# A graph layer with masked attention on one core: nine gathered slots instead of ten, two PSUM banks for the sorting step, and a later norm

## The chip, the cores and the metric

The kernel runs on one core of a Trainium2 chip. The metric is device time in microseconds of one execution, smaller is better. A core has five engines that take their instructions in order, each from its own queue: TensorE (PE in the profile, its weight loads PEld), VectorE (DVE), ScalarE (ACT), GpSimd (POOL) and SyncE (SP). Transfers are issued from SP, ACT and POOL.

## The reference

Two layers over 4096 nodes with 512 features; `adj` is 4096 x 4096, with a full diagonal and otherwise 0.2% of entries that are not zero, all below one.

```python
# layer 0
a = adj + eye
d = sum(a, axis=1) ** -0.5
out = relu((d[:, None] * a * d[None, :]) @ x @ W.T + b)
x = layernorm(x + out)
# layer 1: attention over the neighbours of adj
scores = q @ k.T * kd ** -0.5 + 0.01 * eye - 1e16 * (1 - max(adj, eye))
x = layernorm(x + softmax(scores) @ v @ Wo)
```

In layer 1 every entry of `adj` below one is pushed down by at least 1e16 times its distance from one, so the softmax falls on the diagonal alone, as long as no edge weight reaches one and q, k are not huge. Then layer 1 is `layernorm(x + x @ (Wv Wo))`.

## The kernel before

The function `few_edges_below_one` computes this short form and a flag `bad`, which is one where its conditions do not hold (an edge of weight one or more, a row with more edges than its tables take, large keys). Where `bad` is set, a second function, `general`, computes everything densely; the branch is at L414 and L415.

The 4096 rows are 32 row tiles of 128. **First pass** (loop over `t`, up to `first.close()`): each row tile of `adj` (2 MB) is loaded once; ACT sums its rows (L682); PE computes `x @ W.T` (L675), ACT scales it by `d` (L702) and POOL writes it to DRAM as `y` (L704). VectorE begins to extract the edges: for each of eight segments of 512 columns the eight largest values and their places (MAX8 at L731, FIND_INDEX8 at L732), then a chain of short instructions (L735 to L793) that leaves up to K = 24 edges of every row in a record `rec`. Twelve `early` tiles and five `resident` ones are extracted from the first load; the other fifteen (`again`) are loaded a second time during the second pass, when a buffer of the pool `big` is free (`reload`, L535).

**Sorting step** (`match_key` to `match_end`). A row has some 8 edges, but some have 21. The second pass gathers KH = 10 rows of `y` per row, so a row with more edges lends them to lanes of rows with few. The rows of a tile are put in order of their number of edges: a key per row (L808/L810), a transpose of the key by PE (`match_across`, L815), a count of the keys above (`match_ranks`, L822 on ACT in the second pass, L824 before), permutation matrices (`match_perm`, L832, one for the row itself and one for each of the routes), small products that move the fields of the records (`match_move`, L840 for the row itself, L843 for each route), and `match_end` (L851 to L858), which adds the parts up into columns `cols_all` and weights `wr_all`. Keys and moved fields share one PSUM tile, `bank`, made once: columns 0 to 127 for the key, the next 70 for the fields. The dictionary in the loop tells at which slot `k` of an iteration each stage is issued.

**Second pass** (loop over `i`, 30 tiles of ten slots, then the last two). For each slot POOL gathers 128 rows of `y` (`gather`, L1057, an indirect DMA of 256 KB, AHEAD = 18 slots ahead), ACT builds a 128 x 128 matrix from the weights (`spread`: L955, L959 for the far slots, L965, L968 for the `SAME` = 5 near ones), and PE multiplies (L1265; each fp32 product shows as two records). The last two tiles (`SUMMED`) add their near slots up first (`presum`) and use fewer products (L1084). `own_part` (L1115, ACT) and `own_bias` (L1119) add the diagonal and the bias; `scaled` (L1126) and `residual` (L1137) give the tile's layer 0 output. Then, by the tables `near` and `far` in `at` (tiles behind, slot): T transposes (L663) and copies to SBUF (L668), M multiplies with `Wv Wo` (L675), Q sums squares (L1145), V adds the variance (L1156) and, for two tiles together, takes the power -1/2 on POOL (L1164), F scales (L1170) and writes the result from ACT's queue (L1171). `load_own` (L1067, L540) loads a tile's own rows of `y` and `x` on SP, two tiles ahead, in three buffers.

```python
        far = {"T": (2, 0), "M": (2, 6), "Q": (3, 1), "V": (3, 4), "F": (3, 8)}
                match(*{1: (RANKS,), 3: (MOVE, PERM), 6: (END,), 7: (KEY,), 9: (ACROSS,)}.get(k, ()))
```

The order of the source is not wholly that of the engines: instructions of different chains are placed on an engine when the program is built, and extraction, which nothing else holds back, is placed ahead of the pace that the loop sets (`shares`, 28 tiles). PSUM has eight banks: two for transposes (`pt`), one `bank`, five accumulators (`acc`).

Of the kernel before, what the change touches and what calls it, by code (L numbers as in the profile page):

```python
# [9 lines left out]
FP = mybir.dt.float32  # L10
# [409 lines left out]
def few_edges_below_one(  # L420
# [32 lines left out]
    KH = 10  # L453

    ROUTES = ((112, 10, 14), (120, 14, 19), (76, 19, 24))
    SAME = KH - max(hi - lo for _, lo, hi in ROUTES)

# [9 lines left out]
    ps_a = ctx.enter_context(tc.tile_pool(name="ps_a", bufs=5, space=bass.MemoryType.PSUM))  # L467
# [34 lines left out]
    for n, (c, _, _) in enumerate(ROUTES):  # L502
        ranks(sources[:, n + 1, : c + 1], -2, 2 * c + 1 - P)
        ranks(sources[:, n + 1, c + 1 :], -2, P - 1)
# [205 lines left out]
    def extraction(t, a_t, rec):  # L710
# [35 lines left out]
        def drop(f, r):  # L746
# [19 lines left out]
                lambda: nc.scalar.activation(  # L766
                    mask, keyf[:, 0], AF.Sign, accum_out=n_all[:, t : t + 1]
                ) if second else nc.vector.tensor_scalar(
                    mask, keyf[:, 0], 0.0, 0.0, op0=ALU.is_gt, op1=ALU.add,
                    accum_out=n_all[:, t : t + 1],  # L770
                ),
# [28 lines left out]
    bank = ps_t.tile([P, 512], FP, name="bank", bufs=1)  # L800
# [12 lines left out]
    def match_across(key):  # L813
        pk = bank[:, :P]
        tc.keep_in_program_order(nc.tensor.transpose(pk, key.to_broadcast([P, P]), ident))  # L815
        return pk
# [18 lines left out]
    def match_move(rec, perm):  # L835

        r = upper(rec)
        merged = bank[:, P : P + 7 * KH].rearrange("p (f k) -> p f k", f=7)
        tc.keep_in_program_order(
            nc.tensor.matmul(merged, perm[:, 0], r[:, :, :KH], start=True, stop=False)  # L840
        )
        for n, (_, lo, hi) in enumerate(ROUTES):
            nc.tensor.matmul(  # L843
                merged[:, :, KH - (hi - lo) :], perm[:, n + 1], r[:, :, hi - 1 : lo - 1 : -1],
                start=False, stop=(n == len(ROUTES) - 1),
            )
        return merged

    def match_end(t, merged):
        wr = wr_all[:, t]  # L850
        nc.vector.tensor_copy(wr[:, 0:3], merged[:, 0:3])  # L851
        nc.vector.tensor_tensor(wr[:, 0:3], wr[:, 0:3], merged[:, 3:6], ALU.add)
        nc.vector.tensor_tensor(wr[:, 1], wr[:, 1], merged[:, 6], ALU.add)
        nc.vector.tensor_scalar(cols_all[:, t], wr[:, 0], float(N - 1), None, op0=ALU.min)
        if second:
            nc.scalar.activation(wr[:, 3], wr[:, 1], AF.Copy, scale=-1.0)
        else:
            nc.vector.tensor_scalar(wr[:, 3], wr[:, 1], -1.0, None, op0=ALU.mult)  # L858
# [188 lines left out]
    AHEAD = 18  # L1047
# [14 lines left out]
    def load_own(i):  # L1062
        if i >= NT:
            return
        t = order[i]
        yo[i] = p2.tile([P, D], FP, name="yo", bufs=3)
        nc.sync.dma_start(yo[i], y[ts(t, P), :])  # L1067
        xs[i] = load_x(t, nc.sync, p2, 3)
# [42 lines left out]
    def own_part(i):  # L1111
        t = order[i]
        own = own_all[:, t : t + 1]
        d = d_all[:, t : t + 1]
        nc.scalar.activation(own, own, AF.Identity, scale=d, bias=d)  # L1115
# [15 lines left out]
    def residual(i, c=slice(0, D), part=0):  # L1131
        if i % 2 == 0 and i not in sts:
            sts[i] = small.tile([P, 2, 5], FP, name="sums")
            sts[i + 1] = sts[i][:, 1]
            pairs[i] = sts[i]
            sts[i] = sts[i][:, 0]
        nc.vector.scalar_tensor_tensor(  # L1137
            hs[i][:, c], hs[i][:, c], 0.0, xs[i][:, c], op0=ALU.max, op1=ALU.add,
            accum_out=sts[i][:, part : part + 1],
        )  # L1140
# [19 lines left out]
    def power(i, n):  # L1160

        j = i % 2
        st = pairs[i - j][:, j : j + n]
        nc.gpsimd.tensor_tensor(  # L1164
            st[:, :, 4], st[:, :, 3], mhalf.to_broadcast([P, n]) if n > 1 else mhalf, ALU.pow
        )
# [39 lines left out]
    yo, zs, hs, pts, hTs, ws, sts, pairs, mats, halves = ({} for _ in range(10))  # L1206
# [4 lines left out]
    load_own(1)  # L1211
    own_part(0)
# [8 lines left out]
    def at(step, i, k):  # L1221

        near = {"T": (1, 5), "M": (1, 8), "Q": (2, 2), "V": (2, 3), "F": (2, 7)}
        far = {"T": (2, 0), "M": (2, 6), "Q": (3, 1), "V": (3, 4), "F": (3, 8)}
        for table, tiles in ((near, range(NT - 2, NT)), (far, range(NT - 2))):
            behind, place = table[step]
            if k == place and i - behind in tiles:
                return i - behind
        return None

    for i in range(NT + 2):
# [5 lines left out]
        for k in range(KH):  # L1237
            ends = p == NT - 1
            t = at("T", i, k)
            if t not in (None, NT - 1):  # L1240
                hTs[t] = evacuate(p2, "hT", transpose_rows(hs[t]))
            t = at("M", i, k)
            if t not in (None, NT - 1):
                ws[t] = times(hTs.pop(t), wvo)
            if i == NT - 1:
# [3 lines left out]
                if k == 7:  # L1249
                    scaled(i, HALVES[0])  # L1250
                    residual(i, HALVES[0])
                if k == 8:
                    pts[i] = transpose_rows(hs[i], (0, 1))
                if k == 9:
                    for n in range(KH - SAME + 1):
                        summed_products(i, n, HALVES[1])
                    hTs[i] = p2.tile([P, ND, P], FP, name="hT", bufs=2)
                    nc.scalar.copy(
                        hTs[i][:, 0:2].rearrange("p c s -> p (c s)"), pts[i][:, : 2 * P]
                    )  # L1260
# [11 lines left out]
            if i + 1 in SUMMED and k >= 5:  # L1272
                presum(i + 1, k - 5)
# [15 lines left out]
            if k == 2:  # L1289
                load_own(i + 2)  # L1290
            if k == 3 and i + 1 < NT:
                own_part(i + 1)
            t = at("Q", i, k)
            if t is not None:
                squares(ws[t], D**-0.5, sts[t][:, 3:4])

            t = at("V", i, k)
            if t is not None:
                variance(t)
                if t >= NT - 2:  # L1300
                    power(t, 1)
                elif t % 2:
                    power(t - 1, 2)
            if k == 6 and i < NT:
                own_bias(i)
            if k == 6 and has_p:
                eps_var(p)
            t = at("F", i, k)
            if t is not None and (t >= NT - 2 or t % 2):
                if t < NT - 2:  # L1310
                    finish(t - 1)
                finish(t)
            if k in (3, 9):
                scan_half()
            if staged[KEY] < NT - 2:
                match(*{1: (RANKS,), 3: (MOVE, PERM), 6: (END,), 7: (KEY,), 9: (ACROSS,)}.get(k, ()))
            elif k % 2:
                match(*ALL)
            if k == 9 and queue and len(reloaded) < free:
                reload()  # L1320
            while k == 1 and i + 2 < NT and order[i + 2] not in matched:
# [33 lines left out]
```

## Time and profile before

| | us |
|---|---|
| median of three runs | 749.92 (746.94 to 760.13) |
| the profiled execution | 746.64 |
| its span, first to last instruction | 744.8 |
| PE busy in the span | 591.2 |
| VectorE busy | 545.4 |
| ACT busy | 525.2 |
| POOL busy | 393.2 |

The span is one execution, and all durations are from it. "Busy" is the time in which an engine has an instruction under way; instructions that only wait, branch or issue a transfer do not count. A group's line shows its source line, engine, operation, what it writes and reads, its count, then busy time and mean duration in ns, then the idle time of the engine just before its instructions and who ended most of that. A wait is named after the semaphore that came last, and "issue" or "remote" stands where the records do not tell it. The profile was taken over 744.8 us in which 230.5 MB were moved, 310 GB/s on average.

### The profile page before, as it was taken

How to read it: one execution, taken by the hardware profiler on the slowest of the kernel's cores; microseconds unless marked ns; L12 is line 12 of the kernel's file. 1: busy time of each engine (PE TensorE's matmuls, PEld its weight loads, DVE VectorE, ACT ScalarE, POOL GpSimd, SP SyncE). 2: the span in 40 equal slices, each digit the busy share in tenths (PEclk: the TensorE clock that was granted, in tenths of full speed). 3: DMA queues.
4: the chain of work that ended last, by engine and by line, in shares of the span. 5: the costliest groups of instructions: out<-in, count | busy, mean ns of one | idle time of the engine just before them, and what ended most of it. 6: DMA issues, size and time to landing. Idle time of an engine off the chain costs nothing. (4 is left out here: it accounts for less than half of the span.)

```text
span 744.8 us, 8023 instructions
## 1 busy us (share of the span) xinstructions
PE 591.2 (79%) x1638; PEld 273.9 (37%) x1638; DVE 545.4 (73%) x2109; ACT 525.2 (71%) x1152; POOL 393.2 (53%) x494
## 2 busy tenths in 40 slices
PE   1799959867815687989979699979996789898692
PEld 0444424433302233434434344434442334343350
DVE  6779899999997289889978799959994443322410
ACT  1787798958975287688958597867884887773432
POOL 3224233322337656766666666666665566667500
PEclk9999999999967778999999899999998899999896
DMA  8999999999947689999999988989996577777601
GB/s 341 403 422 426 425 423 406 421 430 413 423 187 262 198 294 366 343 371 373 380 305 343 325 300 313 337 297 333 351 333 209 171 221 239 224 240 248 199 24 62
DMA packets 54411, 230.54 MB, mean 310 GB/s; under 512 B 8592, under 2 KB 9616, under 8 KB 48080
## 3 DMA queue, kind: packets, MB, share of 16 engines
q0 software_dynamic: 30800, 100.95, 40.6%
q1 hardware_dynamic: 18416, 119.55, 40.5%
q10 hardware_dynamic: 5136, 9.44, 3.4%
q14 instruction: 44, 0.36, 0.1%
q8 instruction: 15, 0.25, 0.1%
HBM read 213.12 MB, written 16.78 MB: 309 GB/s over the span
## 5 line engine op out<-in xcount | busy, mean ns | idle before, releaser
L1057 POOL DMA_INDIRECT g<-y,cols_all x320 | 312.9, 978 | 151.0 <-issue 82.6
L1265 PE MATMUL acc<-g,s_t 128*128 128x512 f32 x600 | 283.6, 619 | 20.0 <-ACT s_t L959 20.0
L731 DVE MAX8 v_all<-a_t 128x8 f32<-128x512 f32 x256 | 168.8, 679 | 18.1 <-DMA a_t<-in_adj_dram 18.1
L732 DVE FIND_INDEX8 idx<-v_all,a_t 128x8 uint32<-128x512 f32 x256 | 174.0, 683 | 0.0
L1265 PEld LDWEIGHTS acc<-g,s_t 128*128 128x128 f32 x600 | 116.2, 200 | 151.9 <-issue 124.4
L675 PE MATMUL acc<-wvo,hT 128*128 128x512 f32 x256 | 125.4, 630 | 25.4 <-issue 14.8
L675 PE MATMUL acc<-wT,xT 128*128 128x512 f32 x256 | 121.7, 621 | 16.4 <-ACT xT L668 12.2
L687 ACT ACTIVATE dump<-a_t 128x2048 uint8<-128x2048 f32 (+1 forms) x52 | 119.5, 2297 | 0.0
L675 PEld LDWEIGHTS acc<-wvo,hT 128*128 128x128 f32 x256 | 49.1, 200 | 87.6 <-issue 71.9
L675 PEld LDWEIGHTS acc<-wT,xT 128*128 128x128 f32 x256 | 48.3, 198 | 72.3 <-issue 50.2
L955 ACT ACTIVATE sq<-cols,wr_all 128x128 f32<-128x128 f32 x192 | 66.9, 391 | 9.9 <-issue 7.3
L959 ACT ACTIVATE s_t<-sq,wr_all 128x128 f32<-128x128 f32 x160 | 72.0, 483 | 1.6 <-ACT sq L955 1.2
L968 ACT ACTIVATE s_t<-s_t,wr_all 128x128 f32<-128x128 f32 x150 | 52.4, 391 | 4.6 <-issue 3.8
L682 ACT ACTIVATE dump<-a_n 128x4096 uint8<-128x4096 f32 x15 | 54.5, 3632 | 0.3 <-DMA a_n<-in_adj_dram 0.3
L744 DVE MAX8 top<-key 128x8 f32<-128x64 f32 x192 | 39.0, 214 | 12.1 <-issue 7.3
L1119 DVE SCALAR_TENSOR_TENSOR yo<-yo,own_all,b_bc 128x512 f32<-128x512 f32 x32 | 23.8, 744 | 24.1 <-DMA yo<-y 10.4
L1126 DVE SCALAR_TENSOR_TENSOR h<-acc,d_all,yo 128x512 f32<-128x512 f32 (+1 forms) x33 | 23.9, 724 | 23.5 <-PE acc L1265 11.3
L540 POOL DMA_DIRECT2D x_t<-in_x_dram x32 | 17.9, 564 | 41.2 <-PE pt L663 41.0
L694 POOL TENSOR_SCALAR deg<-deg_all 128x1 f32<-128x1 f32 x32 | 6.7, 220 | 62.4 <-ACT dump L682 62.3
L704 POOL DMA_DIRECT2D y<-y_t x32 | 19.0, 593 | 38.6 <-ACT y_t L702 38.1
L702 ACT ACTIVATE y_t<-acc,d_all 128x512 f32<-128x512 f32 x32 | 21.6, 686 | 22.6 <-POOL d_all L697 16.7
L815 PE MATMUL bank<-ident,rank_key 128*128 128x128 f32 x32 | 10.2, 320 | 33.4 <-issue 11.5
(123 smaller groups left out, 651.5 us busy)
## 6 DMA issues: line engine op xcount, KB each, us to landing
a_t<-in_adj_dram SPq DMA_DIRECT2D x30, 2048.0 KB
a_n<-in_adj_dram SPq DMA_DIRECT2D x15, 2048.0 KB
x_t<-in_x_dram POOLq DMA_DIRECT2D x32, 256.0 KB
y<-y_t POOLq DMA_DIRECT2D x32, 256.0 KB
yo<-y SPq DMA_DIRECT2D x32, 256.0 KB
x_t<-in_x_dram SPq DMA_DIRECT2D x32, 256.0 KB
out_dram<-r_t ACTq DMA_DIRECT2D x32, 256.0 KB
g<-y,cols_all POOLq DMA_INDIRECT x320
```

The source lines that it names most:

```text
L675: nc.tensor.matmul(u, srcT[:, dc, :], w[:, dc, :], start=(dc == 0), stop=(dc == ND - 1))
L682: nc.scalar.activation(dump[:, : part.shape[1]], part, AF.Copy, accum_out=dst)
L687: nc.scalar.activation(dump[:, o], a_t[:, o], AF.Relu, scale=-1.0, accum_out=neg_all[:, t, halves[0] : halves[0] + 1],)
L731: long.append(lambda o=o, seg=seg: nc.vector.max(v[:, o], seg))
L732: long.append(lambda o=o, seg=seg: nc.vector.max_index(idx[:, o], v[:, o], seg))
L744: return lambda: nc.vector.max(top[:, f, r * 8 : r * 8 + 8], keyf[:, f])
L955: nc.scalar.activation(sq, cols1, AF.Square, bias=wr[:, 2, k : k + 1])
L959: nc.scalar.activation(s_t[:, k, :], away(), AF.Relu, scale=wr[:, 3, k : k + 1], bias=wr[:, 1, k : k + 1],)
L968: nc.scalar.activation(s_t[:, k, :], s_t[:, KH, :], AF.Copy, scale=wr[:, 1, k : k + 1])
L1057: nc.gpsimd.indirect_dma_start(out=slots[j], out_offset=None, in_=y[:, :], in_offset=bass.IndirectOffsetOnAxis(ap=cols_all[:, t, k : k + 1 ...
L1126: nc.vector.scalar_tensor_tensor(hs[i][:, c], zs[i][:, c], d_all[:, order[i] : order[i] + 1], yo[i][:, c], op0=ALU.mult, op1=ALU.add,)
L1265: nc.tensor.matmul(zs[i], mats[i][:, k, :], slots.pop(i * KH + k), start=(k == 0), stop=(k == KH - 1),)
```

## The change

KH goes from ten to nine, with a new table of routes: four routes instead of three, each made of runs of lanes (first lane, last lane, rank of the row that fills the first) instead of one start lane. The matrices `sources` are filled accordingly. The shared `bank` becomes two tiles in a bank each, `pk` and `pm`, and the accumulators go from five banks to four. Three small ACT operations go to VectorE. The norm's power is taken for each tile, and the last step (F) follows an iteration later; other steps move by a slot or more, with the copy (E) apart from the transposes (T), and the variance's first part (S) in the table. Own rows are loaded three tiles ahead, in four buffers. The lines on `HALVES` and on the last iterations that only follow the shorter tile are left out below.

```diff
-    KH = 10
-    ROUTES = ((112, 10, 14), (120, 14, 19), (76, 19, 24))
-    SAME = KH - max(hi - lo for _, lo, hi in ROUTES)
+    KH = 9
+    ROUTES = (
+        (9, 13, ((62, 79, 54), (82, 89, 36), (91, 94, 28), (96, 96, 24), (99, 101, 23),
+                 (104, 107, 20), (110, 112, 16), (114, 127, 13))),
+        (13, 16, ((63, 65, 10), (66, 68, 13), (74, 75, 15), (80, 81, 7), (95, 95, 5), (97, 98, 4),
+                  (102, 103, 2), (108, 108, 0))),
+        (16, 20, ((61, 61, 4), (66, 66, 2), (90, 90, 1), (109, 109, 3), (113, 113, 0))),
+        (20, 24, ((109, 109, 0),)),
+    )
+    SAME = KH - max(hi - lo for lo, hi, _ in ROUTES)
...
-    ps_a = ctx.enter_context(tc.tile_pool(name="ps_a", bufs=5, space=bass.MemoryType.PSUM))
+    ps_a = ctx.enter_context(tc.tile_pool(name="ps_a", bufs=4, space=bass.MemoryType.PSUM))
...
-    for n, (c, _, _) in enumerate(ROUTES):
-        ranks(sources[:, n + 1, : c + 1], -2, 2 * c + 1 - P)
-        ranks(sources[:, n + 1, c + 1 :], -2, P - 1)
+    nc.gpsimd.memset(sources[:, 1:], float(P))
+    for n, (_, _, runs) in enumerate(ROUTES):
+        for a, b, r in runs:
+            ranks(sources[:, n + 1, a : b + 1], -2, 2 * r + 1 - P)
...
-                lambda: nc.scalar.activation(
-                    mask, keyf[:, 0], AF.Sign, accum_out=n_all[:, t : t + 1]
-                ) if second else nc.vector.tensor_scalar(
-                    mask, keyf[:, 0], 0.0, 0.0, op0=ALU.is_gt, op1=ALU.add,
-                    accum_out=n_all[:, t : t + 1],
-                ),
+                one(mask, keyf[:, 0], 0.0, 0.0, op0=ALU.is_gt, op1=ALU.add,
+                    accum_out=n_all[:, t : t + 1]),
...
-    bank = ps_t.tile([P, 512], FP, name="bank", bufs=1)
...
-        pk = bank[:, :P]
+        pk = ps_t.tile([P, 512], FP, name="pk", bufs=1)[:, :P]
...
-        merged = bank[:, P : P + 7 * KH].rearrange("p (f k) -> p f k", f=7)
+        pm = ps_t.tile([P, 512], FP, name="pm", bufs=1)
+        merged = pm[:, : 7 * KH].rearrange("p (f k) -> p f k", f=7)
...
-        if second:
-            nc.scalar.activation(wr[:, 3], wr[:, 1], AF.Copy, scale=-1.0)
-        else:
-            nc.vector.tensor_scalar(wr[:, 3], wr[:, 1], -1.0, None, op0=ALU.mult)
+        nc.vector.tensor_scalar(wr[:, 3], wr[:, 1], -1.0, None, op0=ALU.mult)
...
-    AHEAD = 18
+    AHEAD = 16
...
-        yo[i] = p2.tile([P, D], FP, name="yo", bufs=3)
+        yo[i] = p2.tile([P, D], FP, name="yo", bufs=4)
         nc.sync.dma_start(yo[i], y[ts(t, P), :])
-        xs[i] = load_x(t, nc.sync, p2, 3)
+        xs[i] = load_x(t, nc.sync, p2, 4)
...
-        nc.scalar.activation(own, own, AF.Identity, scale=d, bias=d)
+        nc.vector.tensor_scalar(own, own, 1.0, d_all[:, t : t + 1], op0=ALU.add, op1=ALU.mult)
...
-    def power(i, n):
-        j = i % 2
-        st = pairs[i - j][:, j : j + n]
-        nc.gpsimd.tensor_tensor(
-            st[:, :, 4], st[:, :, 3], mhalf.to_broadcast([P, n]) if n > 1 else mhalf, ALU.pow
-        )
+    def power(i):
+        st = sts[i]
+        nc.gpsimd.tensor_tensor(st[:, 4:5], st[:, 3:4], mhalf, ALU.pow)
...
+    load_own(2)
...
-        near = {"T": (1, 5), "M": (1, 8), "Q": (2, 2), "V": (2, 3), "F": (2, 7)}
-        far = {"T": (2, 0), "M": (2, 6), "Q": (3, 1), "V": (3, 4), "F": (3, 8)}
+        near = {"T": (1, 5), "E": (1, 5), "M": (1, 8), "S": (1, 6), "Q": (2, 2), "V": (2, 3), "F": (2, 7)}
+        far = {"T": (2, 0), "E": (2, 3), "M": (2, 7), "S": (2, 1), "Q": (3, 0), "V": (3, 3), "F": (4, 3)}
...
             if k == 2:
-                load_own(i + 2)
+                load_own(i + 3)
...
-            if k == 6 and i < NT:
+            if k == 4 and i < NT:
                 own_bias(i)
-            if k == 6 and has_p:
-                eps_var(p)
+            for t in at("S", i, k):
+                eps_var(t)
...
-                match(*{1: (RANKS,), 3: (MOVE, PERM), 6: (END,), 7: (KEY,), 9: (ACROSS,)}.get(k, ()))
+                match(*{2: (RANKS,), 4: (MOVE,), 5: (PERM, KEY), 8: (ACROSS, END)}.get(k, ()))
...
-            while k == 1 and i + 2 < NT and order[i + 2] not in matched:
+            soon = i + 3 if (i, k) == (NT - 4, KH - 1) else i + 2
+            while k in (1, KH - 1) and soon < NT and order[soon] not in matched:
                 some(count[0] + 1)
                 match(*ALL)
```

## The prediction

> **What bounds it now.** I read the page's first part, then the busy time by stretch. The bounds of the stretches come from the timeline: every twentieth L1265 product starts a row tile, so 228.3 us is the first product, 285.1 that of tile 3, 554.7 that of tile 21, 704.4 the end of tile 29. Columns: stretch, its length, busy time of each engine, granted clock, DMA share, GB/s.
>
> ```profile
> 0.00:228.30 228.30, 161.44 (x497) 78.20 (x497) 209.06 (x872) 171.44 (x172) 72.91 (x163) 0.95 0.96 392
> 228.30:285.10 56.80, 38.98 (x88) 17.29 (x89) 34.79 (x123) 29.18 (x78) 37.73 (x39) 0.80 0.78 262
> 285.10:554.70 269.60, 241.30 (x652) 108.98 (x652) 238.23 (x872) 212.57 (x593) 181.07 (x187) 0.96 0.94 336
> 554.70:704.40 149.70, 123.22 (x321) 55.09 (x320) 56.94 (x221) 100.40 (x284) 98.41 (x103) 0.93 0.72 222
> 704.40:744.80 40.40, 26.23 (x86) 14.35 (x84) 6.39 (x24) 11.56 (x28) 3.11 (x5) 0.86 0.16 55
> ```
>
> The first pass is a transfer (DMA 0.96). In the 476.1 us from 228.3 to 704.4 PE leads: 403.5 us busy, 72.6 idle, 15.9 per tile. In the longest stretch VectorE is close behind (13.2 us a tile to PE's 13.4, of 15.0); afterwards it is nearly idle, because extraction (L731, L732) is done at 578. Then PE's own waits after 222 us (total, times, longest); and below them three groups by form (busy, mean ns | idle before):
>
> ```profile
> PE bank L815 <- issue: 11.5, 3, 6.7
> PE bank L815 <- DVE wr_all L853: 6.9, 2, 4.5
> PE bank L815 <- ACT dump L1145: 6.2, 1, 6.2
> PE bank L815 <- DVE idx L732: 4.7, 1, 4.7
> PE bank L840 <- ACT above L822: 3.7, 2, 2.2
> PE bank L840 <- issue: 2.6, 1, 2.6
> PE bank L815 <- DVE v_all L731: 1.7, 1, 1.7
> ```
> ```profile
> L1057 POOL DMA_INDIRECT g<-y,cols_all x320 | 312.9, 978 | 151.0 <-issue 82.6 <-PE acc L1265 34.4 <-remote 14.1
> L1265 PE MATMUL acc<-g,s_t 128*128 128x512 f32 x600 | 283.6, 619 | 20.0 <-ACT s_t L959 20.0
> L832 DVE TENSOR_SCALAR perm<-sources,rank 128x512 bf16<-128x512 bf16 x32 | 11.5, 359 | 13.3 <-issue 10.2 <-ACT s_t L965 2.5 <-ACT above L822 0.5
> ```
>
> L815 sums to 31.0 us; L840, with three smaller rows (1.2, 1.1, 1.0), to 9.6. So 40.6 of the 72.6 us that PE stands idle end at the two instructions that write the tile `bank`. At 283.95 the key transpose starts right after VectorE's last read of the *other* half of that bank (L853, 283.74); everything behind it on PE, products included, stood 4.46 us. Gathers aren't the limit: POOL waits 34.4 us for PE to free a slot, PE 6.2 us for a gather.
>
> **What the skill says.** PSUM — Partial Sum Buffer, "PSUM bank collisions raise a hardware error": two engines are kept apart by bank, not by address; that is the wait just shown. TensorE: Matmul & The Clock Gate, Part 1: an idle window of about 3.4 us halves the clock; the trace agrees (0.80 granted where the 4 to 7 us waits lie, 0.96 later). SBUF — State Buffer, "Who interferes with whom": VectorE in a two-port mode and GpSimd lock each other out. The trace hints at it: after `perm` at 418.20 and 569.21 VectorE starts nothing for 4.1 and 4.6 us while gathers issue; in other places nothing follows.
>
> **The change, part by part.**
>
> *Nine slots.* 60 fewer L1265 records at 283.6/600 = 0.473 us: −28.4 us of PE work, 0.95 a tile; the two summed tiles lose a slot each (L1084, 2 records of 0.44 and 4 of 0.24): −2 in the tail. POOL loses 32 gathers of 0.98 + 0.30 issue (−41 us); ACT 32 × (391 + 483 ns) = −28; the DMA engines 32 × 262 kB = 8.4 of 230 MB. PE is the bound, so the 28.4 counts; the rest is hidden behind PE today. 16 instead of 18 gathers ahead is 1.8 tiles either way. Counting the reference's rows (at most 21 edges beside the diagonal) through the new table, every edge finds a free slot and none is hit twice, so the `general` branch isn't taken.
>
> *Fourth route.* One more small product (L843, 0.19 us, 0.04 to 0.06 apart in a run) per tile: +2 on PE. `perm` grows from 512 to 640 columns: 359 × 5/4 = +0.09 us. 16 more iotas (seven took 1.10 us) and a memset (0.2): POOL's first x load goes 2.7 us later than 3.39, hidden, since x is first transposed after W's second transposes (20.5); uncovered it would cost 2.7.
>
> *Two banks.* Takes the cause of the 40.6 us away. PE then waits at L815 only for the key and for ACT's reading of the last one (L822), at L840 for `perm` and L853. New places (PERM a slot behind MOVE, END four slots behind MOVE instead of three) leave more room. Bounds: all 40.6 and some 10 us of clock, or 10 if VectorE is late in its place. Price paid: accumulators 5 to 4. In the loop's order a bank for the second product (M, i−2 at slot 7) is the one that r_t of tile i−4 frees at slot 3: four slots of 1.4 us. In the first pass PE waits 3.9 us for ACT today; the DMA share of 1.00 (to 206 us) hides it: 0, at most +4.
>
> *ACT to VectorE.* own_part (32 × 378 ns on ACT; 0.20 on VectorE by its one-column rows), mask (18 × 0.28), sign (24 × 0.19), `perm`: 6.4 + 5.0 + 4.6 + 2.9 = +19 us on VectorE, 0.6 a tile. It ends VectorE's waits for ACT (own 8.8, mask 8.5). In the long stretch VectorE would need 13.8 us a tile. Own and sign may be two-port operations, some 55 more beside the 72 of today (`perm`, L851, L854); three of those were followed by 2.5 to 4.6 us of nothing, so +3 to +10; I take 3, as part falls in the idle stretch.
>
> *Norm later, one tile at a time.* T stays, the hT copy comes three slots later (ACT waited 20.6 us for the products ahead of it), M one later, final scale 4 tiles behind. POOL: 30 powers of 0.556 for 15 of 0.749, +5.5 us against −41. A power waits for VectorE's variance with the gathers queued behind it (11.4 us before 705); the gathers' lead of 16 covers that. Output transfers are the same, only the last two tiles set the end, and theirs stay near: 0.
>
> *Own rows.* Two 256 KB loads a tile, a tile earlier, a buffer more. SP's queue is in order: from 223.8 to 262.9 it waits for VectorE's h with the first reload behind. The fourth load now goes at once, so reloads may start up to 15 us sooner; they aren't on the path (one 1.6 us wait for a_t after 228). VectorE's waits for yo (10.4 us, three) mostly end. One more pair at the start competes with the first gathers: 0.5 MB at 300 GB/s (estimate from the second stretch), +1 to +2, taken +1.
>
> **Sum by stretch.** First 56.8: slots 2.8, half of its three bank waits (4.7 + 6.7 + 4.5): −11. Long stretch: the most VectorE allows at 13.8 is 18 × 1.2 = 21, and 6 more if extraction, which the compiled order ran ahead, spreads into the idle stretch: −27. Third: slots 8.5, bank 3, hT and own rows 2.5: −14. Tail −2, start +1, locks +3. Total −50: 746.6 − 50 = **697 us**. That is against the profiled execution (746.64, span 744.8); it stood 3.3 below the median of the runs (749.92), so I expect the median at 697 to 700 and give 697.
>
> **Rivals.**
> - *All of it* (0.22): bank waits wholly gone, clock back. 746.6 − 28.4 − 40.6 − 10 + 2 − 2 + 3 = 670. For: VectorE idles 93 of 150 us in the third stretch, POOL's floor is 288 × 1.28 + 17 = 386. Against: VectorE's order.
> - *The wait moves to VectorE* (0.22): the long stretch stays VectorE's, L851 still waits in its line for the moved fields; only the slots count where PE leads. 746.6 − 28 + 3 = 722. For: 88% busy and 0.6 a tile more.
> - *Within 2%* (0.07): the same with a slow start and more locks, about 740.
> - *The accumulators* (0.05, slower): r_t waits for POOL's power (12.0 us in four waits, up to 6.3). If it comes over four slots (5.8 us) late, PE stops at M. To eat 50 us over 28 tiles it must be 1.8 + 5.8 = 7.6 us late each time; at 9 us, 28 × 3.2 = 90: 697 + 90 = 787.
> - My forecast has 0.44, its own range 680 to 714.
>
> The range 663 to 729 leaves out the accumulators, most of the within-2% case and the edges of the first two. About 2% is what a measurement of this kernel can tell from no change (limits 735 and 765): faster 0.86, same 0.09, slower 0.05.
>
> **What would show it.** PE's L815 and L840 waits together under 12 us; 540 L1265 records and about 254 us busy; 288 gathers; VectorE over 13.5 us a tile in the long stretch, with extraction ending later in tiles than 21; PE's clock above 0.9 in the second stretch. It is wrong if acc L675 waits for r_t, if L815 now waits as long for the key, or if VectorE's idle gaps beside gathers multiply.

## The result and the profile after

The changed kernel takes 718.5 us (median of four runs, 714.9 to 724.8) beside 753.7 us of the kernel before (four runs, 746.9 to 760.1): a ratio of 0.957, 95% interval 0.944 to 0.970. It is faster, by 35 us of medians; the profiled executions differ by 22 us (spans 744.8 and 722.9), since the one of after (724.8) is the longest of its runs and the one of before (746.6) as short as the shortest of its own. A ratio leaves out every run over 1.5% above the fastest of its kernel, so it is not the quotient of the medians.

One thing has to be said before any wait is read. The kernels of this study ran in five groups, each beside the kernel before, and the kernel before was not equally fast in them: 753.7 us in the first pair, 758.3 in one group, 708.4, 708.5 and 710.2 in three. So runs are compared by their ratio to the kernel before of their own group, and times only between groups in which that kernel took the same. Repeated in a group at 708.4, the changed kernel took 666.7 us: ratio 0.9425 (0.936 to 0.949).

First the stretches of the profile after (stretch, its length, busy time of PE, PEld, DVE, ACT, POOL, clock, DMA share, GB/s), cut where the same tiles begin as in the table of the prediction: first product, tile 3, tile 21, end of tile 29.

```profile
0.00:235.70 235.70, 166.38 (x505) 80.53 (x506) 215.94 (x893) 171.01 (x169) 74.31 (x179) 0.93 0.93 378
235.70:288.20 52.50, 37.58 (x83) 15.73 (x84) 24.99 (x102) 29.46 (x73) 35.38 (x37) 0.81 0.82 280
288.20:548.20 260.00, 228.82 (x633) 102.23 (x632) 224.48 (x888) 197.26 (x507) 170.40 (x180) 0.95 0.91 335
548.20:684.80 136.60, 112.94 (x310) 49.60 (x309) 78.43 (x295) 83.95 (x224) 85.61 (x91) 0.95 0.67 210
684.80:722.90 38.10, 24.82 (x81) 13.17 (x78) 7.44 (x27) 10.80 (x27) 6.12 (x8) 0.91 0.20 67
```

The four stretches of the second pass became 4.3, 9.6, 13.1 and 2.3 us shorter; the first pass became 7.4 us longer. In the 30 full tiles (from the first product to the end of tile 29) PE's work fell by 24 us and its standing hardly at all (72.5 to 69.4). PE's waits in the same profile show where it stood (total, times, longest):

```profile
PE acc L684 <- ACT hT L677: 29.3, 10, 6.5
PE acc L684 <- issue: 6.7, 5, 3.7
PE pm L845 <- DVE wr_all L858: 6.1, 1, 6.1
PE pk L819 <- issue: 5.7, 1, 5.7
PE acc L684 <- ACT rank_key L812: 4.1, 1, 4.1
PE acc L684 <- DVE h L1127: 3.9, 1, 3.9
```

The key transpose (L819) and the moved fields (L845), which PE waited 40.6 us for, now cost 13.2 (with one row of 1.4 that is not shown). But the product with Wv Wo (L684, L675 before) waits 47.5 us, in the four rows here and one of 3.5, where the trace before shows 24.7 of it (14.8, 5.1, 3.8, 1.0). Of the 27.4 us that one kind of wait gave up, another took 22.8. The groups that the prediction counted on: 540 product records with 255.2 us, 288 gathers, and `perm`, which takes 389 ns where I had worked out 449.

```profile
L1059 POOL DMA_INDIRECT g<-y,cols_all x288 | 281.8, 978 | 116.7 <-issue 66.9
L1261 PE MATMUL acc<-g,s_t 128*128 128x512 f32 x540 | 255.2, 610 | 21.7 <-DMA yo<-y 14.1
L836 DVE TENSOR_SCALAR perm<-sources,rank 128x640 bf16<-128x640 bf16 x32 | 12.4, 389 | 2.3 <-issue 1.3 <-ACT above L826 1.0
```

### The profile page after: what moved, and what is told of

It reads as the page before. It is cut to its first block, busy times and chain, and to the rows that moved or that the text cites. A ratio compares the mean times of both kernels' runs of the same rounds, so it can differ in the third digit from the quotient of the medians.

```text
span 722.9 us, 7843 instructions
## 1 busy us (share of the span) xinstructions
PE 570.5 (79%) x1604; PEld 261.3 (36%) x1604; DVE 551.3 (76%) x2201; ACT 492.5 (68%) x996; POOL 371.8 (51%) x494
## 3 DMA queue, kind: packets, MB, share of 16 engines
q0 software_dynamic: 28240, 92.56, 37.2%
## 5 line engine op out<-in xcount | busy, mean ns | idle before, releaser
L1059 POOL DMA_INDIRECT g<-y,cols_all x288 | 281.8, 978 | 116.7 <-issue 66.9
L1261 PE MATMUL acc<-g,s_t 128*128 128x512 f32 x540 | 255.2, 610 | 21.7 <-DMA yo<-y 14.1
L684 PE MATMUL acc<-wvo,hT 128*128 128x512 f32 x256 | 133.0, 667 | 48.2 <-ACT hT L677 29.3
L1261 PEld LDWEIGHTS acc<-g,s_t 128*128 128x128 f32 x540 | 99.7, 194 | 133.0 <-issue 124.8
L684 PE MATMUL acc<-wT,xT 128*128 128x512 f32 x256 | 126.2, 643 | 26.1 <-ACT xT L677 16.8
L684 PEld LDWEIGHTS acc<-wvo,hT 128*128 128x128 f32 x256 | 52.6, 213 | 124.6 <-issue 69.3
L684 PEld LDWEIGHTS acc<-wT,xT 128*128 128x128 f32 x256 | 50.4, 205 | 86.7 <-issue 55.4
L957 ACT ACTIVATE sq<-cols,wr_all 128x128 f32<-128x128 f32 x160 | 58.4, 391 | 16.8 <-DVE wr_all L857 8.8
L961 ACT ACTIVATE s_t<-sq,wr_all 128x128 f32<-128x128 f32 x128 | 58.9, 483 | 0.2 <-ACT sq L957 0.2
L1160 POOL TENSOR_TENSOR sums<-sums,mhalf 128x1 f32<-128x1 f32 x32 | 20.2, 631 | 67.6 <-DVE sums L1154 59.0
L1143 ACT ACTIVATE dump<-acc 128x512 f32<-128x512 f32 x32 | 18.8, 588 | 50.4 <-PE acc L684 15.2
L970 ACT ACTIVATE s_t<-s_t,wr_all 128x128 f32<-128x128 f32 x150 | 46.8, 389 | 0.0
L1127 DVE SCALAR_TENSOR_TENSOR h<-acc,d_all,yo 128x512 f32<-128x512 f32 (+1 forms) x33 | 23.7, 719 | 22.8 <-remote 13.7
```

The lines of the kernel that those rows point to most:

```text
L684: nc.tensor.matmul(u, srcT[:, dc, :], w[:, dc, :], start=(dc == 0), stop=(dc == ND - 1))
L957: nc.scalar.activation(sq, cols1, AF.Square, bias=wr[:, 2, k : k + 1])
L961: nc.scalar.activation(s_t[:, k, :], away(), AF.Relu, scale=wr[:, 3, k : k + 1], bias=wr[:, 1, k : k + 1],)
L970: nc.scalar.activation(s_t[:, k, :], s_t[:, KH, :], AF.Copy, scale=wr[:, 1, k : k + 1])
L1059: nc.gpsimd.indirect_dma_start(out=slots[j], out_offset=None, in_=y[:, :], in_offset=bass.IndirectOffsetOnAxis(ap=cols_all[:, t, k : k + 1 ...
L1127: nc.vector.scalar_tensor_tensor(hs[i][:, c], zs[i][:, c], d_all[:, order[i] : order[i] + 1], yo[i][:, c], op0=ALU.mult, op1=ALU.add,)
```

## The experiments

Theory at the outset: the slots give some 28 us and the separate banks 27; the banks' gain is partly given back, because the hT copy (the transposed tile, copied from PSUM to SBUF for the product with Wv Wo) stands on ScalarE behind the rank key, which now waits for a mask on VectorE, and because there is an accumulator less. The rival: only the slots count, and the banks merely moved a wait. The table has the profiled executions of all that follows, cut at the first product and the end of tile 29; "stands" is the time between these two in which PE neither multiplies nor loads weights. The last two columns are the median of the runs and the ratio to the kernel before of the group.

| kernel | first product | PE works | PE stands | rest | span | median | ratio |
|---|---|---|---|---|---|---|---|
| before, first pair | 228.4 | 403.5 | 72.5 | 40.5 | 744.8 | 753.7 | 1 |
| after, first pair | 235.7 | 379.7 | 69.4 | 38.1 | 722.9 | 718.5 | 0.957 |
| before, again | 228.2 | 392.2 | 35.4 | 46.3 | 702.1 | 708.4 | 1 |
| after, again | 236.3 | 364.9 | 27.4 | 37.6 | 666.3 | 666.7 | 0.9425 |
| slots only | 231.0 | 363.6 | 24.6 | 45.5 | 664.8 | 663.2 | 0.935 |
| banks only | 234.8 | 393.7 | 36.1 | 45.3 | 709.9 | 713.5 | 1.008 |
| after, one bank, five accumulators | 229.9 | 363.9 | 30.6 | 35.6 | 659.9 | 664.5 | 0.939 |
| after, one bank, four | 233.7 | 366.9 | 27.3 | 37.2 | 665.1 | 667.9 | 0.944 |
| after, operations on ACT | 235.5 | 367.8 | 28.7 | 36.7 | 668.6 | 671.4 | 0.949 |
| after, key on VectorE | 236.4 | 365.1 | 29.7 | 37.4 | 668.6 | 669.8 | 0.945 |
| one bank, own rows back | 228.5 | 379.0 | 59.1 | 37.1 | 703.7 | 707.5 | 0.951 |
| one bank, order back | 227.9 | 373.7 | 58.2 | 36.4 | 696.2 | 700.4 | 0.938 |
| slots and operations | 227.5 | 369.5 | 58.6 | 44.7 | 700.4 | 706.5 | about 0.94 |
| slots and single power | 229.2 | 363.1 | 25.7 | 35.8 | 653.8 | 657.7 | 0.928 |

### Banks and accumulators put back

```diff
-        pk = ps_t.tile([P, 512], FP, name="pk", bufs=1)[:, :P]
+        pk = bank[:, :P]
-        pm = ps_t.tile([P, 512], FP, name="pm", bufs=1)
-        merged = pm[:, : 7 * KH].rearrange("p (f k) -> p f k", f=7)
+        merged = bank[:, P : P + 7 * KH].rearrange("p (f k) -> p f k", f=7)
-    ps_a = ... name="ps_a", bufs=4
+    ps_a = ... name="ps_a", bufs=5
```

> The changed kernel with the shared bank for keys and moved fields and the fifth accumulator put back, all else as changed. Theory A (the separate banks took away 40.6 - 13.2 = 27.4 us of TensorE's waits, and the fourth accumulator in their place gave some of it back as waits of the product with Wv Wo): 718.5 + 27 - 11 = about 735, with waits at the key transpose and the moved fields of 25 us or more again and none of that product for VectorE's release of a bank. Theory B (the nine slots did it all, VectorE's line sets the pace and the banks only moved a wait): 715 to 722, with the same waits then standing in TensorE's slack.

The second version of this has the same edit without the last line, so four accumulators.

> The changed kernel with the shared bank, but with four accumulators as changed. Against the version with shared bank and five accumulators it shows what the fifth accumulator is worth by itself. Theory A (the fourth accumulator costs the product with Wv Wo the 11.4 us that it waits for VectorE's release): about 11 us above that version, so near 746. Theory B (those waits are slack that another wait would take): the same within 3 us.

Measured: 664.5 us (661.8 to 664.9), ratio 0.939 (0.932 to 0.947), and with four accumulators 667.9 (667.0 to 668.3). The kernel before took 708.5 us in this group, so 735 us, theory A's number on the first pair's scale, would be a ratio of 0.975, and theory B's 715 to 722 one of 0.949 to 0.958. The measured one lies below both: putting the bank back costs nothing, and PE waits only 3.1 us at it in the trace of the first version. The fifth accumulator is worth 3.4 us by time (no run of one version reaches a run of the other), a third of what theory A gave it.

### Three operations back on ScalarE, and the key moved to VectorE

```diff
-                one(mask, keyf[:, 0], 0.0, 0.0, op0=ALU.is_gt, op1=ALU.add,
-                    accum_out=n_all[:, t : t + 1]),
+                lambda: nc.scalar.activation(mask, keyf[:, 0], AF.Sign, accum_out=n_all[:, t : t + 1]) ...
-        nc.vector.tensor_scalar(own, own, 1.0, d_all[:, t : t + 1], op0=ALU.add, op1=ALU.mult)
+        nc.scalar.activation(own, own, AF.Identity, scale=d, bias=d)
-        nc.vector.tensor_scalar(wr[:, 3], wr[:, 1], -1.0, None, op0=ALU.mult)
+        nc.scalar.activation(wr[:, 3], wr[:, 1], AF.Copy, scale=-1.0) ...
```

> The changed kernel with the three small operations (the diagonal's part, the mask, the sign) back on ScalarE in the second pass. Theory A (ScalarE's line stands still at the rank key, which now waits for VectorE's mask, and the copy of hT stands behind it, so that TensorE's product with Wv Wo waits 34.8 us for the copy, 10 more than before): those waits fall to 25 us or less, about 708 to 712. Theory B (ScalarE was the one to be relieved, 16 us of work, and VectorE bears it): 718 to 724. Theory C (VectorE is the bound and is relieved by 16 us): 703 to 710, and then the version with only the key moved to VectorE must not gain.

```diff
-        if second:
-            nc.scalar.activation(key, n, AF.Identity, scale=-float(P), bias=row0n)
-        else:
-            nc.vector.tensor_scalar(key, n, -float(P), row0n, op0=ALU.mult, op1=ALU.add)
+        nc.vector.tensor_scalar(key, n, -float(P), row0n, op0=ALU.mult, op1=ALU.add)
```

> The changed kernel with the rank key computed on VectorE too, so that ScalarE no longer waits for VectorE's mask ahead of its own work; VectorE gets some 20 short operations more (about 2 us), ScalarE as many less. Theory A (the wait of ScalarE's line for the mask is what holds the copy of hT): TensorE's waits for that copy fall from 34.8 us to under 25, time 706 to 713. Theory C (VectorE's work is the bound): 718 to 722, not faster.

Measured: 671.4 us (669.2 to 673.8), ratio 0.949 (0.941 to 0.958), and 669.8 us (665.9 to 670.7), ratio 0.945 (0.937 to 0.953). Beside the first pair's 0.957 both would look like gains. Beside the changed kernel repeated at the same level (below: 666.7 us, 666.3 to 668.2, the kernel before at 708.4 there and at 708.5 here) neither is a gain: the medians are 4.8 and 3.1 us above it (all runs of the first lie above it, those of the second overlap). So neither theory A (ScalarE's line waits for the mask) nor theory C (VectorE is the bound) holds there: as far as two groups can be compared (the intervals of the ratios overlap), ScalarE was well relieved of the three operations, and VectorE bears them.

### The two kernels again, and the parts alone

The changed kernel and the kernel before, unedited:

> The changed kernel itself, beside its versions of the first group, whose kernel before took 708.5 us there and not 753.7. Theory A (the separate banks are worth some 16 us net): a ratio to the kernel before of 0.92, below the 0.939 of the version with shared bank and five accumulators. Theory B (the banks are worth nothing where the sorting step's waits have other cover; the slots did it): 0.94 to 0.955, so the same as that version. A trace in which the waits of the product with Wv Wo are again 34.8 us speaks for a cause in the program; one in which they are under 15 says that they came from the execution, not from the order of the program.

> The kernel before itself, for its trace beside the changed one's on the same chip. If the 40.6 us of waits at the two writers of the shared bank are the program's, they stand here again within a few us. If they belong to the execution that was profiled first, they are under 15 us here, the second pass is some 40 us shorter (about 436 instead of 476 us from the first product to the end of the last full tile) and the busy times of the engines are the same.

The changed kernel took 666.7 us, ratio 0.9425 (0.936 to 0.949): theory B. The kernel before took 703.9 us in the profiled execution. These are PE's waits in it, from 215 us on, at the bank and for the copy:

```profile
PE acc L675 <- ACT hT L668: 19.4, 8, 8.7
...
PE bank L840 <- ACT above L822: 6.4, 3, 5.1
PE bank L840 <- DVE top L744: 3.2, 1, 3.2
...
PE bank L815 <- ACT rank_key L808: 0.6, 1, 0.6
```

The bank's waits are 10.2 us, not 40.6; PE stands 35.4 us in the 30 tiles, not 72.5. In the changed kernel's trace of this group the product with Wv Wo waits 8.8 us for the hT copy, not 29.3:

```profile
PE acc L1261 <- DMA g<-y,cols_all: 19.2, 17, 3.7
...
PE acc L684 <- ACT hT L677: 8.8, 3, 4.8
```

So most of both lists was not the program's. In both kernels it is the same program with the same sequence on every engine (on VectorE of the changed one 2201 records, the same line and operation at each place). What is left of the changed kernel's standing, 27.4 us, is for the larger part a wait for gathered rows: 19.2 us, where the kernel before waits 8.8. The prediction held that gathers are not the limit; here they are the largest wait.

The slots alone: the new table, the filling of `sources`, KH = 9, AHEAD = 16 and what follows from the shorter tile, all else as before.

> The kernel before with nine slots, the four routes and 16 gathers ahead alone; shared bank, five accumulators, order, norm, own rows and ScalarE's operations as before. Theory B (the slots are the gain): 28.4 us of TensorE's work less 2 for the route, 26 us, a ratio of 0.96 to 0.965 of a kernel before at 708 us, so over two thirds of what the changed kernel gains. Rival (VectorE is the bound in the long stretch, and the slots only count in the 12 tiles where it is not): 12 x 0.95 = 11 us, 0.98 to 0.985.

The two banks alone:

> The kernel before with the two tiles pk and pm in a bank each and four accumulators instead of five, nothing else. Theory A (the shared bank costs TensorE its 40.6 us): a ratio of 0.945 to 0.975. Theory B (the waits are not the bank's or have no share in the time): 0.99 to 1.01. If the fourth accumulator is what hurts: above 1.01.

The slots alone give 663.2 us (657.1 to 666.7), ratio 0.935 (0.927 to 0.943): all that the whole change gains, and more than the 0.96 to 0.965 that was expected of them. Of the 37.3 us between the spans 28.6 are PE's work in the full tiles and 10.8 its standing, less 2.0 (the start is 2.8 later, the rest 0.8 shorter); the medians differ by 45.2, as the profiled execution of before lies 4.5 below its group's median and that of the slots 3.5 above its own. The rival that gave the slots 11 us falls.

The banks alone are a loss of 0.8% (1.005 to 1.010, some 5 us), with this in PE's waits:

```profile
PE acc L1265 <- ACT r_t L1170: 14.8, 4, 10.2
PE acc L675 <- ACT hT L668: 11.3, 4, 5.7
```

There is no wait at `pk` or `pm` any more, but the first product of a tile waits for a bank that the final scale (L1170) has still to read.

### Own rows, order, and operations, each on a smaller version

Three versions to find where the late first product and the shorter end come from. Shared bank, five accumulators, and own rows as before (bufs=3, `load_own(i + 2)`, no `load_own(2)`):

> The changed kernel with the shared bank and five accumulators, and the own rows loaded two tiles ahead in three buffers as before. Theory A (the later first product, 236.3 us against 228.2, is the third pair of own rows in front of the gathers): first product 3 to 6 us sooner than the 229.9 of the version with only the bank put back, time 659 to 662. Theory B (the later first product is the four accumulators' in the first pass, as the 229.9 and 233.7 us of the versions with five and four say): first product 229 to 231 again. If the sooner own rows are what makes the end after the last full tile 35.6 us instead of 46.3, that end is 43 us or more here and the time 671 or more.

Shared bank, five accumulators, and the table for the far tiles as before:

```diff
-        far = {"T": (2, 0), "E": (2, 3), "M": (2, 7), "S": (2, 1), "Q": (3, 0), "V": (3, 3), "F": (4, 3)}
+        far = {"T": (2, 0), "E": (2, 0), "M": (2, 6), "S": (2, 1), "Q": (3, 1), "V": (3, 4), "F": (3, 8)}
```

> The changed kernel with the shared bank and five accumulators, and the table for the far tiles as before (copy of hT at T, M at slot 6, Q, V and F an iteration sooner), with the power still taken for each tile. Theory A (the later order only moves work that lies beside the path): 662 to 667, as the 664.5 of the version with the bank alone put back. Theory B (the later order is what takes the waits for hT away): waits of the product with Wv Wo for the copy of hT rise from 7.1 to some 20 us, as in the version with the slots alone, and the time to 672 or more. Theory C (the later order costs, since the version with the slots alone has full tiles 6 us shorter): 657 to 661.

The kernel before with the slots and the three operations on VectorE:

> The kernel before with the nine slots and the three small operations on VectorE, all else as before. Theory A (the operations on VectorE gain what the changed kernel lost when they were put back, 671.4 - 666.7 = 4.8 us): 656 to 660, and with that faster than the changed kernel. Theory B (VectorE is full until extraction ends, and 11.6 us more of it delay that end and the tiles behind): 666 to 671.

Measured: 707.5, 700.4 and 706.5 us beside 758.3 of the kernel before in this group, ratios 0.951 (0.936 to 0.965), 0.938 (0.919 to 0.957) and about 0.94 (from two runs of each kernel, with no interval). The intervals are too wide to rank the three, so the times settle nothing, and the theories on the later order and on the operations stay open; the traces settle two things. The first product comes at 228.5, 227.9 and 227.5 us, so own rows a tile sooner don't delay it (theory B of the first). And the rest after the last full tile stays 36 to 37 us with own rows back or order back, and is 44.7 in the version that takes powers in pairs. The waits at the shared bank are large again in this group: 41.8, 38.9 and 46.1 us. In the version with the order back the waits of the product with Wv Wo for the copy are 16.2; PE stands 58.2 us in it, less than the 69.4 of the changed kernel with its separate banks in the first pair.

### The slots and the single power

```diff
-                if t >= NT - 2:
-                    power(t, 1)
-                elif t % 2:
-                    power(t - 1, 2)
+                power(t, 1)
-            if t is not None and (t >= NT - 2 or t % 2):
-                if t < NT - 2:
-                    finish(t - 1)
+            if t is not None:
```

> The kernel before with the nine slots alone, and the norm's power taken for each tile as in the changed kernel, with the final scale in its old place; shared bank, five accumulators, own rows and ScalarE's operations as before. Theory A (a pair's power stands behind six or seven gathers on GpSimd, and two final scales and the copy of hT stand behind it on ScalarE, which makes the end after the last full tile 45 us in the versions with pairs and 36 to 38 in those without): an end of 36 to 39 us instead of 45.5, a ratio of 0.920 to 0.928 beside the 0.935 of the slots alone and the 0.9425 of the changed kernel. Theory B (the shorter end comes from the order of the sorting step or from the operations on VectorE): an end of 44 to 46 us and a ratio of 0.93 to 0.94.

Measured: 657.7 us (653.6 to 660.3) beside 710.2, ratio 0.928 (0.922 to 0.933), the fastest version here and below the whole changed kernel's 0.9425 (0.936 to 0.949), each against its own group; the rest after the last full tile is 35.8 us instead of 45.5. These are theory A's numbers; beside the slots alone (0.927 to 0.943) the ratios overlap, and it is the rest that tells. All nine profiles with a power for each tile have a rest of 35.6 to 38.1 us, the five with pairs 40.5 to 46.3. The timelines of the two versions show what changed (start, length, engine, line, what; in brackets the idle time before). The slots alone, whose last full tile ends at 619.2:

```profile
625.69 0.95 POOL L1066 DMA_INDIRECT g<-y,cols_all  x1 [0.30 <-DVE sums L1165]
626.66 0.73 POOL L1173 TENSOR_TENSOR sums<-sums,mhalf 128x2 f32<-128x2 f32 x1
627.42 1.27 ACT L1179 ACTIVATE r_t<-acc,sums 128x512 f32<-128x512 f32 x2 [5.80 <-POOL sums L1173]
...
629.73 2.93 PE L684 MATMUL acc<-wvo,hT 128*128 128x512 f32 x3 [5.75 <-ACT hT L677]
```

With a power for each tile, the last full tile ending at 618.0:

```profile
620.67 0.57 POOL L1173 TENSOR_TENSOR sums<-sums,mhalf 128x1 f32<-128x1 f32 x1
621.28 0.69 ACT L1179 ACTIVATE r_t<-acc,sums 128x512 f32<-128x512 f32 x1 [5.08 <-POOL sums L1173]
...
623.01 3.27 PE L684 MATMUL acc<-wvo,hT 128*128 128x512 f32 x7 [0.29 <-ACT hT L677]
```

In the first, gathers stand one behind another up to 626.6, the pair's power comes behind them, two final scales behind the power and the copy (629.1) behind those; PE waits 5.75 us at the end of the chain, and its eight products then take 6.75 us. In the second the power comes 2.7 us after the last full tile instead of 7.5, PE waits 0.3, and the eight products take 3.70. Theory A's reason is not borne out, though: the variance on VectorE (L1165) that the power needs ends only at 625.4 in the first and at 618.4 in the second, so the gathers in front of the power held it 1.2 us there and 2.2 here. The variance of the pair's other tile was done at 612.8 and waited for this one. Why this one comes so late is not shown.

## Why the prediction was right, and where not

I gave 697 us (663 to 729) and faster by over 2% with 0.86; 718.5 lies in the range, and the direction is right. The size was 50 us; the profiled executions of the first pair give 22, medians 35, the repeat 42. By stretch the sum said -11, -27, -14, -2 in the tail and +1 at the start; the profile of the first pair has -4.3, -9.6, -13.1, -2.3 and +7.4. That the repeat comes so near to 50 is partly luck: the slots gave more than I counted (45 us of medians when alone), the banks none of the 21 that I gave them.

*Nine slots: right, and undercounted.* Foretold were 28.4 us of PE's work; measured are 28.6 alone on the path, and 255.2 us of products in the first pair, where I wrote about 254 (my own figures, 283.6 less 28.4, give 255.2). That other waits also shrink (10.8 us of standing) I did not count. Extraction does spread, as I argued for the long stretch: in the first pair it ends at 604.4 us, in tile 25, beside 578.6 in tile 22 of before, and in the repeat at 555.8 in tile 24, beside 542.2 in tile 21. So VectorE needed only 12.5 us a tile there, not over 13.5. Two of my signs failed: the waits at L819 and L845 are 13.2 us, not under 12, and PE's clock in the second stretch is 0.81, not over 0.9.

*Two banks: the step that failed.* "Takes the cause of the 40.6 us away": some 21 us of my sum (the 8 of the first stretch, 10 of the long one, 3 of the third) rest on it. The waits fell to 13.2 us, but the standing by 3.1. In the repeat the same waits of the kernel before are 10.2 us. By time, the separate banks are worth 1.2 us in the changed kernel (667.9 against 666.7, in two groups at 708.5 and 708.4), which these runs cannot tell from nothing; with the accumulator that they cost they are a loss, about 5 us alone and perhaps 2.1 here (664.5 against 666.7, with intervals that overlap). Of the 40.6 us, 14.1 carry the name "issue", for which the trace names nobody, and I counted them as the bank's. The rest I read so: the sorting step is where PE first needed what ScalarE and VectorE had late in that execution, and with the bank gone, PE needed it at the next place, the product with Wv Wo. The two lists of waits of the first pair agree with this, and so does the group at 758 us, where the shared bank brings 38.9 us of its own waits and no more standing than the separate ones; but these are executions of different groups, so the move is likely and not shown. The sentence that I took from the Trainium skill (PSUM — Partial Sum Buffer, "PSUM bank collisions raise a hardware error") says that accesses are kept apart by bank, and the trace agrees (the key transpose at 283.95 us starts behind VectorE's read of 283.74); it doesn't say that the wait costs time, and I read it so.

*Four accumulators: priced at nothing.* I looked at the second pass, and for the first wrote that the DMA share hides it, "0, at most +4". The first product comes at 227.5 to 231.0 us in all the versions with five (mean of eight profiles 228.8) and at 233.7 to 236.4 in those with four (mean of six 235.4): 6.6 us. In the one pair that differs in nothing else, the two versions of one bank, it is 3.8 us (229.9 and 233.7), at the edge of what I allowed; the other five with four accumulators have the separate banks too, and what adds the rest was not tried. With five accumulators, PE's last products and the last `y`:

```profile
204.48 4.88 PE L684 MATMUL acc<-wT,xT 128*128 128x512 f32 x11
...
220.53 0.54 POOL L713 DMA_DIRECT2D y<-y_t  x1 [0.41 <-ACT y_t L711]
```

With four:

```profile
199.34 0.69 ACT L711 ACTIVATE y_t<-acc,d_all 128x512 f32<-128x512 f32 x1 [1.91 <-DMA y<-y_t]
...
202.34 0.69 ACT L711 ACTIVATE y_t<-acc,d_all 128x512 f32<-128x512 f32 x1 [2.32 <-DMA y<-y_t]
...
214.25 5.40 PE L684 MATMUL acc<-wT,xT 128*128 128x512 f32 x8 [2.82 <-ACT y_t L711]
...
224.88 0.54 POOL L713 DMA_DIRECT2D y<-y_t  x1 [0.41 <-ACT y_t L711]
```

The accumulators hold `x @ W.T` until the row tile's degree is known. With one less, PE falls behind: it stands before its last products until ScalarE has read an accumulator at 214.2, and they end at 219.7 us instead of 209.4. The last `y` leaves 4.35 us later, and every gather waits for that `y`. But that delay is older than PE's wait: ScalarE stands 1.9 and 2.3 us at 199.3 and 202.3, by the trace for transfers of earlier `y`, and from there on it sums rows and scales with few pauses, all of it later by that. The six profiles with four accumulators have these two waits, the eight with five have no such wait after 175 us. How the accumulators bring them about is not shown.

The rival that made the accumulators decide by way of r_t was far too large, but its mechanism exists: 14.8 us of waits for r_t in the version with the banks alone.

*Own rows: priced at one, and nothing found.* The 7.4 us of the start, of which I gave own rows one, aren't theirs. In the first pair the trace names "DMA yo<-y" for them, the last of several semaphores; the version with own rows back starts no sooner (228.5) than the one of its group with them (227.9).

*Norm: the tail was missed.* I set it at 0, "only the last two tiles set the end, and theirs stay near". The power for each tile shortens the rest by 9.7 us: the copy of the next tile no longer stands behind a late power and two final scales. In the first pair little of this is seen: there the pair's power came 0.7 us after the last full tile, and the rest fell only from 40.5 to 38.1. The later order of F gave nothing that a run here can tell.

*Operations to VectorE: probably the wrong sign.* The +3 for locks rested on the Trainium skill (SBUF — State Buffer, "Who interferes with whom"), by which VectorE in a two-port mode and GpSimd block each other, and on three gaps behind such operations in the trace of before. Putting the operations back costs 4.8 us, between two groups, so whatever locks there are come to less than ScalarE's relief. And the gaps don't speak for locks: that trace has seven behind such operations, not three, but 20 more of over a microsecond behind others, and in the repeat of the same program there is none (last section). No run here measures a lock by itself.

Of my rivals, "the wait moves to VectorE" gave 722, close to the 718.5, and its core (only the slots count) held; its reason did not, since no run shows that the operations on VectorE cost anything. Against my 697, the profiled 724.8 is 28 more: some 20 from standing that stayed, 6 from the start.

Still open is why the kernel takes 754 to 758 us in two groups and 708 to 710 in three, and so how much the banks are worth where VectorE and ScalarE are late. The number of the chip doesn't tell the two apart: the group at 758.3 and the one at 710.2 are recorded under the same one. What differs in the traces is in the last section; no run told one cause from another.

## What to carry to other kernels

A list of waits from one execution says where an engine stood, not what made it stand; before a resource is given up to remove a wait, ask which wait would take its place, and look whether the list is the same in a second execution and how much of it is put down to nobody. What a buffer is worth is asked in every pass that draws from its pool, above all at the end of a pass, where the transfer that covered it is over. And an operation that serves two tiles at once waits for the later one: look at what stands behind it when the last tiles run.

## What the runs showed of the hardware that was not expected

The kernel before, with the same order of its records on every engine, ran 42.7 us apart (spans 744.8 and 702.1) at nearly the same busy times of three engines: VectorE 545.4 and 542.8 us, ScalarE 525.2 and 524.0, GpSimd 393.2 and 393.9. The first passes end alike (228.4 and 228.2). In the full tiles PE stands 37.1 us longer and works 11.3 longer, at a granted clock of 0.93 instead of 0.96; the rest is 5.8 shorter.

One sign tells the two kinds of execution apart. In the full tiles of the slower one VectorE waits 70.4 us, in 25 waits, for which the trace names no engine and no transfer ("issue" and "remote"). The largest group of them:

```profile
DVE sums L1156 <- issue: 11.8, 4, 4.7
```

In its repeat there is no such wait. The changed kernel has 47.0 us of them in the first pair and none in the repeat, the three versions of the group at 758 us have 34.6 to 45.4, and of the seven other versions one has a single wait of 7.4 us and six have none. They belong to no one instruction: seven of the 27 gaps of over a microsecond that nobody else ended in the slower execution follow `perm`, L851 or L854, the others MAX8, FIND_INDEX8 and more. Nor do they follow the gathers in time: GpSimd has one under way in 65% of the time of these gaps, and in 65% of the full tiles as a whole.

One chain of VectorE in the changed kernel, in the first pair:

```profile
605.15 0.08 DVE L744 DVE_READ_ACCUMULATOR own<-idx,spot,v_all 128x1 f32 x1
607.23 0.23 DVE L744 SCALAR_TENSOR_TENSOR key<-idx,place 128x64 uint32<-128x64 uint32 x1 [2.00 <-remote]
...
609.38 0.23 DVE L744 SCALAR_TENSOR_TENSOR key<-v_all,key 128x64 uint32<-128x64 uint32 x1 [1.79 <-remote]
```

and in the repeat:

```profile
556.53 0.08 DVE L744 DVE_READ_ACCUMULATOR own<-idx,spot,v_all 128x1 f32 x1
556.53 0.22 DVE L744 SCALAR_TENSOR_TENSOR key<-idx,place 128x64 uint32<-128x64 uint32 x1
...
556.88 0.21 DVE L744 SCALAR_TENSOR_TENSOR key<-v_all,key 128x64 uint32<-128x64 uint32 x1
```

From the first of these to the last it is 4.23 us in one and 0.35 in the other, with nothing in the chain that another engine had to deliver. What holds such instructions was not tried, and the cause is open.
